# Turning attention probabilities with transposing DMAs, as two 16-bit planes, in a decoder layer on one core

## The chip, the core and the metric

The kernel runs on one core of a Trainium2 chip. The metric is the device time of one launch in microseconds (us). A core has TensorE (PE in the profile), VectorE (DVE), ScalarE (ACT), GpSimd (POOL) and SyncE (SP); each works through its own instructions in order, and the engines wait for each other through semaphores. DMAs are issued by an engine's queue and moved by 16 DMA engines that all queues share.

## The reference, cut to what matters

The program is one decoder layer on x (4 x 512 x 512, float32): a first attention over features, a layer norm, a second attention block, a layer norm, a feed-forward part with ternary weights, and a last layer norm. The change lies in the second block, whose core is this:

```python
def _gqa(q, k, v):
    scale = 1.0 / np.sqrt(q.shape[-1])
    scores = jnp.einsum('bsghd,btgd->bghst', q, k) * scale
    p = jax.nn.softmax(scores, axis=-1)
    return jnp.einsum('bghst,btgd->bsghd', p, v)
```

It is called with 8 groups of 2 heads of width 128 over 512 positions (self-attention), and once more over 64 context positions (cross-attention). Queries and keys come out of linears on 8-bit inputs and a layer norm over each head; both results are divided, rounded to 8-bit values and multiplied by a projection.

## The kernel before, in words

The program has three stages in a row: the first attention with the preparation of the weights, the second block, and the feed-forward part.

**Units and slots.** The second block runs as 16 units: 4 batches times 4 pairs of groups (`u`, lines 1088 to 1130). A unit has 4 heads of 512 query rows, and a head is taken in 4 blocks of 128 rows, so a unit has 16 slots and the block has 256. The whole order of the work is written out by hand: the engines' instructions stand in the order in which the code calls them (only SyncE's DMAs are placed by the scheduler).

**What one slot does for its own block of scores.** `score` (line 818) multiplies 128 query rows with 512 keys into a PSUM tile `ps`, and VectorE takes the row maximum `nm` (line 826). `exponents` (828) lets ScalarE write `p = exp(ps - max)` and the row sums `rsum`. `quotients` (833) takes the reciprocal on VectorE and scales `p` on GpSimd (835). `turn_score` (837), two slots later, turns `p` on TensorE: four transposes of 128 x 128 float32 into a PSUM tile `pt` (line 115, by way of `transpose4`), and ScalarE copies it into `pT` (842). When a head's four blocks are turned, `value` (844) multiplies `pT` with the values in 8 matmuls into `po`, in the third slot of the next head, and `finish` (854) has ScalarE scale the result into a bfloat16 tile `fq_y`, which VectorE rounds to 8-bit values in five steps (lines 207 to 212).

**What else a slot does.** `plan(u)` (1025) puts other work into the slots: the 12 linears of the next unit (`LINEARS`; line 788, 8 or 16 matmuls each), turns of the normalised queries and keys through PSUM (`turn`, line 807, copied by ScalarE in 811), the cross-attention (`CONTEXT`: scores in line 880, its turn, its values in 917), the projection of the unit before (`OUT`, line 946, 8 matmuls each), and, in two of four units, the next batch's inputs (`quantise`, 244). `statistics` (722) and `scale` (735) normalise what the linears left in PSUM: VectorE's statistics, GpSimd's power (109), VectorE's product (740).

**Order on the engines.** In a slot, ScalarE first does the copies that the slot before left in `early`, then the copy of the turned probabilities, then the exponents, then what the plan adds. GpSimd does the quotients and then the powers of `statistics`.

**Buffers.** The PSUM pools hold 4 banks for products, 2 for turns and 2 for scores. The linears' weights come from DRAM in tiles of 512 KB, four to a linear kind (line 773), into 8 buffers, so that a kind's loads start as soon as the kind two before it is done.

Of the kernel before, what the change touches and what calls it, by code (L numbers as in the profile page):

```python
# [28 lines left out]
P = 128  # L29
# [25 lines left out]
def decoder_layer(  # L55
# [79 lines left out]

    fqp = hat = lnp = quants = ps_mm = ps_t = ps_s = None
# [79 lines left out]
    class Inputs:  # L216
# [27 lines left out]
        def quantise(self, w, c0, due=1):  # L244
            def begin():
                if c0 == 0:
                    self.qa[w] = quants.tile([P, KC, S], F32R, name="qa", tag="qa")
                y = fqp.tile([P, 2 * S], BF16, name="fq_y", bufs=4)
                for j in range(2):
                    col = 4 * w + c0 + j  # L250
                    nc.scalar.activation(
                        y[:, j * S : (j + 1) * S], self.lns[c0 + j], AF.Copy,
                        scale=inv_t[:, col : col + 1],
                    )
                round_later(y, self.qa[w][:, c0 : c0 + 2, :].rearrange("p c s -> p (c s)"), due)

            early.append(begin)
# [436 lines left out]
    hatk = wts = qkp = vals = prob = probT = cross = catq = wpp = raws = None  # L694
    turned_as = {0: ("qT", 5), 1: ("qxT", 4), 2: ("kT", 4)}
    parts = 1

    def open_attention(stack, right, wl, v, p, pt, cq, wp, raw):
        nonlocal hat, hatk, wts, qkp, vals, prob, probT, cross, catq, wpp, raws, ps_mm, ps_t, ps_s
        wts = pool_in(right, "wts", wl, **R)  # L700
        qkp = pool_in(stack, "qkp", 4, **L)
        vals = pool_in(stack, "vals", v, **L)
        prob = pool_in(stack, "prob", p, **L)
        probT = pool_in(stack, "probT", pt, **L)
        cross = pool_in(stack, "cross", 2, **L)
        catq = pool_in(stack, "catq", cq, **L)
        wpp = pool_in(stack, "wpp", wp, **L)
        hat = pool_in(stack, "hat", 8 if raw else 4, **L)
        hatk = pool_in(stack, "hatk", 4, **L) if raw else hat
        if raw:  # L710
            raws = pool_in(stack, "raws", 1, **L)
        ps_mm = pool_in(stack, "ps_mm", 4, space=PSUM)
        ps_t = pool_in(stack, "ps_t", 2, space=PSUM)
        ps_s = pool_in(stack, "ps_s", 2, space=PSUM)

    st = ExitStack()
    open_attention(st, right, 8, 10, 4, 1, 6, 1, True)
# [40 lines left out]
    class Unit:  # L758
# [78 lines left out]
        def turn_score(self, i, p):  # L837
            if i == 0:
                self.pT = probT.tile([P, TPB, S], F32, name="pT")
            pt = ps_t.tile([P, 4, P], F32, name="pt", tag="pt")  # L840
            transpose4(pt, p, ident)
            nc.scalar.copy(self.pT[:, :, i * P : (i + 1) * P], pt)  # L842
# [11 lines left out]
        def finish(self, half, j, h, po):  # L854

            if h == 0:
                self.half[half] = fqp.tile([P, 2 * S], BF16, name="fq_y", bufs=4)
# [167 lines left out]
    def plan(u):  # L1025
# [12 lines left out]
        if u == 0:  # L1038
            for j in range(1, 4):
                add(j, me.turn, 0, j)  # L1040
        else:
            add(0, me.turn, 0, 3)
            for j in range(4):
                add(1 + j, me.turn, 1, j)
# [3 lines left out]
        for j, (l, a, t, v) in enumerate(CONTEXT):  # L1048
            add(l, me.load_context, j)
            add(a, me.context_scores, j)  # L1050
            add(t, me.context_turn)
            add(v + (not nxt), me.context_values, j)
        if last:
            if nxt:
                add(1, last.load_out)
            last.pp = {}

            for i, s in enumerate(OUT if nxt else (5, 9)):
                add(s, last.out, i, PAIRS)
# [5 lines left out]
        if me.gp == GP - 2 and b < B:  # L1065
# [3 lines left out]
            quants_at = ((6, 2, 0, 3), (8, 2, 2, 3), (10, 3, 0, 3), (12, 3, 2, 2), (14, 0, 0, 5))  # L1069
        elif me.gp == GP - 1 and b < B:  # L1070
            quants_at = ((2, 0, 2, 3), (4, 1, 0, 3), (7, 1, 2, 3))
# [8 lines left out]
        (0, 2, 0), (1, 2, 1), (3, 2, 2), (5, 2, 3), (7, 0, 0), (8, 0, 1), (9, 0, 2), (11, 0, 3),  # L1080
        (12, 1, 0), (13, 1, 1), (13, 1, 2), (15, 1, 3),
    )
    TURNS = (9, 2, 0), (10, 2, 1), (13, 0, 0), (14, 0, 1), (15, 0, 2)
    CONTEXT = (1, 4, 8, 9), (6, 8, 12, 13)
    OUT = 5, 7, 9, 11
    scored = []
    heads = []
    for u in range(NU):
# [4 lines left out]
        for s in range(16):  # L1093
# [4 lines left out]
            if i == 2 and heads:  # L1098
                me.exponents()
                m, k = heads.pop(0)  # L1100
                m.value(k)
            if len(scored) == 2:
                m, *k = scored.pop(0)
                m.turn_score(*k)
            if i != 2 or u + h == 0:
                me.exponents()
            scored.append((me, i, me.p))
# [5 lines left out]
            me.quotients()  # L1113
            statistics()
            later.run(0.9)
            later.slot += 1
            if u == NU - 1 and s == 0:
# [5 lines left out]
                catq_end = pool_in(right, "catq_end", 4, **R)  # L1123
# [5 lines left out]
            if u == NU - 1 and s == 3:  # L1129
# [4 lines left out]
    for n, (m, *k) in enumerate(scored):  # L1134
        m.turn_score(*k)
        last.out(2 + n, PAIRS)
    later.run(9)
# [178 lines left out]
    with tc.If(rest > 0):  # L1316
# [4 lines left out]
        open_attention(st, st, 4, 4, 2, 1, 2, 2, False)  # L1321
        for b in range(B):
# [9 lines left out]
            for gp in range(GP):  # L1332
# [9 lines left out]
                for j in range(2):  # L1342
                    for h in (2 * j, 2 * j + 1):
                        for i in range(TPB):
# [3 lines left out]
                            me.turn_score(i, me.p)  # L1348
# [89 lines left out]
```

## Time and profile before

| | us |
|---|---|
| median of 3 runs (lowest to highest) | 1772.45 (1772.16 to 1772.91) |
| the profiled execution, its own time | 1770.97 |
| its span, first to last instruction | 1769.1 |
| TensorE busy in the span | 1736.9 |
| VectorE busy | 1216.5 |
| ScalarE busy | 855.6 |
| GpSimd busy | 655.5 |
| first score of the second block starts at | 399.8 |
| granted TensorE clock, mean | 0.998 |

A line of the profile that describes a group of instructions gives the kernel's line, engine, operation, the tiles written and read, the shape, the count after an x, then busy time in us and the mean ns of one, then the idle time of the engine just before them and what ended it. A line of a timeline gives start and length in us, engine, line, operation, tiles, shape and how many follow each other. Matmuls overlap, so what one costs is read from its start to the start of the next. A line of stretches gives, for a piece of the span, each engine's busy time and count, the granted clock, the share of the 16 DMA engines that was busy, and GB/s.

### The profile page before, as it was taken

The page shows a single profiled execution, that of the slowest core. Times are in us where ns is not written, and L with a number is a line of the kernel's source. Part 1 is how long each engine was busy: PE and PEld are TensorE (multiplying, and loading weights), DVE is VectorE, ACT ScalarE, POOL GpSimd, SP SyncE. Part 2 cuts the span into 40 slices and gives each one's busy share as a digit, 9 for nine tenths or more (in the row PEclk, how much of TensorE's full clock was granted, in tenths as well). Part 3 has the DMA queues.
Part 4 walks back from the last instruction along what each step waited for, and adds up shares of the span by engine and source line. Part 5 has one row for each costly group of instructions (what it writes and reads, how often), then busy time and mean ns, then how long its engine had stood idle before and what let it go on. Part 6 is the DMA issues. An engine that isn't in the chain of part 4 may idle for free. (4 is left out here: it accounts for less than half of the span.)

```text
span 1769.1 us, 23876 instructions
## 1 busy us (share of the span) xinstructions
PE 1736.9 (98%) x7874; PEld 1068.3 (60%) x7874; DVE 1216.5 (69%) x2564; ACT 855.6 (48%) x1735; POOL 655.5 (37%) x918
## 2 busy tenths in 40 slices
PE   8999989999999999999999999999999999999997
PEld 4545454466767666666766766666666766644443
DVE  1456666756666886666688676668867675659886
ACT  1445454525545555454555545556554555543221
POOL 1222131333433443343443343334434333326663
PEclk9999999999999999999999999999999999999999
DMA  8768586783433324353232435313342542505543
GB/s 262 225 221 276 158 281 207 231 287 111 134 129 106 123 69 147 115 189 97 103 123 70 148 139 172 137 55 124 104 157 95 172 140 71 201 2 121 122 102 83
DMA packets 161605, 256.91 MB, mean 145 GB/s; under 512 B 60592, under 2 KB 95408, under 8 KB 159424
## 3 DMA queue, kind: packets, MB, share of 16 engines
q1 hardware_dynamic: 160256, 251.06, 43.8%
q0 software_dynamic: 1216, 4.23, 0.8%
q8 instruction: 65, 1.06, 0.2%
q14 instruction: 68, 0.56, 0.1%
HBM read 194.55 MB, written 50.33 MB: 138 GB/s over the span
## 5 line engine op out<-in xcount | busy, mean ns | idle before, releaser
L835 POOL TENSOR_SCALAR p<-p,rsum 128x512 f32<-128x512 f32 x256 | 191.1, 746 | 580.4 <-DVE rsum L834 447.6
L788 PE MATMUL pl<-wl,qa 128*128 128x512 f32 (+1 forms) x2048 | 400.8, 345 | 0.8 <-DVE x L404 0.8
L788 PEld LDWEIGHTS pl<-wl,qa 128*128 128x128 f32 x2048 | 310.2, 189 | 37.0 <-DVE x L404 1.6
L826 DVE TENSOR_REDUCE nm<-ps 128x1 f32<-128x512 f32 x256 | 176.2, 688 | 222.2 <-PE ps L821 222.1
L842 ACT COPY pT<-pt 128x512 f32<-128x512 f32 x256 | 150.5, 588 | 286.8 <-PE pt L115 286.4
L821 PE MATMUL ps<-kT,qT 128*128 128x512 f32 x512 | 265.9, 601 | 4.6 <-ACT p L831 3.7
L831 ACT ACTIVATE p<-ps,nm 128x512 f32<-128x512 f32 x256 | 178.1, 696 | 144.2 <-DVE nm L826 140.6
L109 POOL TENSOR_TENSOR rstd<-rstd,nhalf 128x4 f32<-128x4 f32 (+2 forms) x236 | 226.5, 960 | 19.7
L848 PE MATMUL po<-pT,val 128*128 128x512 f32 x512 | 230.3, 592 | 0.0
L115 PEld LDWEIGHTS pt<-ident,p 128*128 128x128 f32 x1152 | 143.5, 141 | 140.0 <-issue 117.3
L115 PE MATMUL pt<-ident,p 128*128 128x128 f32 x1152 | 172.4, 273 | 1.0 <-POOL p L835 1.0
L848 PEld LDWEIGHTS po<-pT,val 128*128 128x128 f32 x512 | 96.2, 190 | 123.3 <-issue 111.7
L729 DVE BATCH_NORM_STATS2 qk_st<-pl 128x6 f32<-128x256 f32 x320 | 122.8, 419 | 37.5 <-ACT val L796 26.4
L740 DVE TENSOR_TENSOR xn<-pl,rstd 128x512 f32<-128x512 f32 (+1 forms) x192 | 113.3, 595 | 16.9 <-POOL rstd L109 16.5
L946 PE MATMUL pp<-wb,cq 128*128 128x512 bf16 x512 | 121.0, 380 | 0.0
L493 POOL TENSOR_TENSOR wr<-wr,wb 128x512 f32<-128x512 f32 x32 | 38.6, 1207 | 164.6 <-ACT wb L491 118.2
L807 PE MATMUL pt<-ident,xn 128*128 128x128 f32 x640 | 96.1, 273 | 2.9 <-ACT qxT L811 2.6
L821 PEld LDWEIGHTS ps<-kT,qT 128*128 128x128 f32 x512 | 81.5, 190 | 28.4 <-issue 12.6
L1225 ACT ACTIVATE h<-pg,xi_ds 128x512 f32<-128x512 f32 x64 | 43.9, 688 | 109.9 <-PE pg L1220 109.9
L860 ACT ACTIVATE fq_y<-po,inv_t 128x512 bf16<-128x512 f32 x128 | 84.5, 688 | 8.7 <-PE po L848 4.6
L1220 PEld LDWEIGHTS <-xiT 128*128 128x128 bf16 x512 | 50.0, 98 | 61.9 <-issue 1.0
L946 PEld LDWEIGHTS <-cq 128*128 128x128 bf16 x512 | 45.6, 98 | 65.3 <-issue 18.7
(518 smaller groups left out, 2648.7 us busy)
## 6 DMA issues: line engine op xcount, KB each, us to landing
wl<-wl_d SPq DMA_DIRECT2D x192, 512.0 KB, 6.1
wl_d<-wd SPq DMA_DIRECT2D x48, 512.0 KB, 4.4
wb<-wb_d SPq DMA_DIRECT2D x16, 1024.0 KB, 9.5
wr<-in_wproj_dram SPq DMA_DIRECT2D x32, 256.0 KB, 4.5
wr<-in_wgu_dram SPq DMA_DIRECT2D x32, 256.0 KB, 4.8
wr<-in_wqkv_dram SPq DMA_DIRECT2D x32, 256.0 KB, 4.1
raw<-in_wgu_dram SPq DMA_DIRECT2D x32, 256.0 KB, 3.9
tern_d<-tern SPq DMA_DIRECT2D x48, 128.0 KB, 2.2
```

Source lines behind the costliest of these rows:

```text
L109: nc.gpsimd.tensor_tensor(y, y, nhalf[:, :n], ALU.pow)
L115: nc.tensor.transpose(dst[:, c, :], src[:, c * P : (c + 1) * P], idn)
L729: nc.vector.bn_stats(stt[:, 2 * j : 2 * j + 2, :].rearrange("p a b -> p (a b)"), ps[:, 2 * j * D : (2 * j + 2) * D].rearrange("p (h d) -> ...
L740: nc.vector.tensor_tensor(xn, ps[:, : n * D].rearrange("p (h d) -> p h d", h=n), y.unsqueeze(2).broadcast_to([P, n, D]), ALU.mult,)
L788: nc.tensor.matmul(ps[:, at : at + n], lhsT=self.qa[a][:, c, ts], rhs=self.ws[c][:, k, at : at + n], start=(c == 0 and k == 0), stop=(c == ...
L821: nc.tensor.matmul(self.ps, lhsT=self.qT[h][:, i * P : (i + 1) * P], rhs=self.kT[h // 2], start=True, stop=True,)
L826: nc.vector.tensor_reduce(self.nm, self.ps, AX.X, ALU.max, negate=True)
L831: nc.scalar.activation(self.p, self.ps, AF.Exp, bias=self.nm, accum_out=self.rs)
L835: nc.gpsimd.tensor_scalar(self.p, self.p, self.rs, 1.0, ALU.mult, ALU.mult)
L842: nc.scalar.copy(self.pT[:, :, i * P : (i + 1) * P], pt)
L848: nc.tensor.matmul(po, lhsT=self.val[c][:, j * D : (j + 1) * D], rhs=self.pT[:, c, :], start=(c == 0), stop=(c == TPB - 1),)
L946: nc.tensor.matmul(pp, lhsT=q, rhs=w, start=(first and n == 0), stop=(last and n == len(terms) - 1))
```

## The change

The four transposes and their PSUM tile go away for the probabilities. In `quotients`, GpSimd now also copies `p`, read as 16-bit halves, into a tile `p2` with the 512 low halves first and the 512 high halves behind them. `send`, a slot later, is a transposing DMA of the 128 x 1024 16-bit values into `t2`, issued from ScalarE's queue. `receive`, two slots after that, is a ScalarE copy that joins the two planes again in `pT`: 1024 16-bit elements in place of 512 float32. `value` stands in the fourth slot of the next head, where it stood in the third. The plan's slots are laid out anew, and some buffer counts change: weights 8 to 7, values 10 to 11, `p` 4 to 2, `qT` 5 to 4, `kT` 4 to 3, the last projection's inputs 4 to 2. The computation is the same.

```diff
-    turned_as = {0: ("qT", 5), 1: ("qxT", 4), 2: ("kT", 4)}
+    turned_as = {0: ("qT", 4), 1: ("qxT", 4), 2: ("kT", 3)}
...
+        planes = pool_in(stack, "planes", 2 if raw else 1, **L)
...
-    open_attention(st, right, 8, 10, 4, 1, 6, 1, True)
+    open_attention(st, right, 7, 11, 2, 1, 6, 1, True)
...
             nc.gpsimd.tensor_scalar(self.p, self.p, self.rs, 1.0, ALU.mult, ALU.mult)
 
-        def turn_score(self, i, p):
+            self.p2 = planes.tile([P, 2, S], U16, name="p2")
+            nc.gpsimd.tensor_copy(self.p2, self.p.bitcast(U16).rearrange("p (k h) -> p h k", h=2))
+
+        def send(self, p2):
+
+            t2 = planes.tile([P, 2 * TPB, P], U16, name="t2", bufs=3 if parts == 1 else 1)
+            nc.scalar.dma_start(t2, p2.rearrange("p h k -> p (h k)"), transpose=True)
+            return t2
+
+        def receive(self, i, t2):
+
             if i == 0:
                 self.pT = probT.tile([P, TPB, S], F32, name="pT")
-            pt = ps_t.tile([P, 4, P], F32, name="pt", tag="pt")
-            transpose4(pt, p, ident)
-            nc.scalar.copy(self.pT[:, :, i * P : (i + 1) * P], pt)
+            nc.scalar.copy(
+                self.pT[:, :, i * P : (i + 1) * P].bitcast(U16).rearrange("p c (q h) -> p c q h", h=2),
+                t2.rearrange("p (h c) q -> p c q h", h=2),
+            )
...
-            quants_at = ((6, 2, 0, 3), (8, 2, 2, 3), (10, 3, 0, 3), (12, 3, 2, 2), (14, 0, 0, 5))
+            quants_at = ((6, 2, 0, 2), (8, 2, 2, 2), (10, 3, 0, 2), (12, 3, 2, 1), (14, 0, 0, 4))
         elif me.gp == GP - 1 and b < B:
-            quants_at = ((2, 0, 2, 3), (4, 1, 0, 3), (7, 1, 2, 3))
+            quants_at = ((0, 0, 2, 2), (3, 1, 0, 3), (5, 1, 2, 2))
...
     LINEARS = (
-        (0, 2, 0), (1, 2, 1), (3, 2, 2), (5, 2, 3), (7, 0, 0), (8, 0, 1), (9, 0, 2), (11, 0, 3),
-        (12, 1, 0), (13, 1, 1), (13, 1, 2), (15, 1, 3),
+        (0, 2, 0), (1, 2, 1), (2, 2, 2), (4, 2, 3), (5, 0, 0), (6, 0, 1), (8, 0, 2), (9, 0, 3),
+        (10, 1, 0), (12, 1, 1), (13, 1, 2), (14, 1, 3),
     )
-    TURNS = (9, 2, 0), (10, 2, 1), (13, 0, 0), (14, 0, 1), (15, 0, 2)
-    CONTEXT = (1, 4, 8, 9), (6, 8, 12, 13)
-    OUT = 5, 7, 9, 11
+    OWN = (0, 0, 3), (1, 1, 0), (2, 1, 1), (3, 1, 2), (4, 1, 3)
+    TURNS = (7, 2, 0), (11, 2, 1), (13, 0, 0), (14, 0, 1), (15, 0, 2)
+
+    CONTEXT = (1, 5, 10, 14), (9, 13, 18, 20)
+    CONTEXT_END = (1, 5, 9, 10), (6, 9, 13, 15)
+    OUT = 8, 9, 10, 12
     scored = []
+    sent = []
     heads = []
+
+    def move_on():
+        while scored:
+            m, i, p2 = scored.pop(0)
+            sent.append((m, i, m.send(p2)))
...
-            if i == 2 and heads:
-                me.exponents()
+            if i == 3 and heads:
                 m, k = heads.pop(0)
                 m.value(k)
-            if len(scored) == 2:
-                m, *k = scored.pop(0)
-                m.turn_score(*k)
-            if i != 2 or u + h == 0:
-                me.exponents()
-            scored.append((me, i, me.p))
+            me.exponents()
+            arrived = sent[:-1]
+            del sent[:-1]
+            move_on()
+            for m, k, t2 in arrived:
+                m.receive(k, t2)
...
             me.quotients()
+            scored.append((me, i, me.p2))
...
     run_early()
-    for n, (m, *k) in enumerate(scored):
-        m.turn_score(*k)
+    for n in range(2):
+        move_on()
+        m, k, t2 = sent.pop(0)
+        m.receive(k, t2)
         last.out(2 + n, PAIRS)
+    for m, k, t2 in sent:
+        m.receive(k, t2)
     later.run(9)
     me.value(3)
```

A triple of `LINEARS` is (slot, kind, block), where kind 2 gives keys and values, 0 the queries and 1 the cross-attention's queries; `OWN` and `TURNS` are (slot, kind, head). A row of `CONTEXT` gives the slots of its load, scores, turn and values; numbers from 16 up lie in the next unit.

More of the change, by code (lines that the diff above doesn't have):

```diff
@@ L134, in decoder_layer @@
     nc.vector.tensor_copy(ident_h, ident)
+    parts = 1
     fqp = hat = lnp = quants = ps_mm = ps_t = ps_s = None
@@ L247, in begin @@
                     self.qa[w] = quants.tile([P, KC, S], F32R, name="qa", tag="qa")
-                y = fqp.tile([P, 2 * S], BF16, name="fq_y", bufs=4)
+                y = fqp.tile([P, 2 * S], BF16, name="fq_y", bufs=4 if parts == 1 else 2)
                 for j in range(2):
@@ L691, in decoder_layer @@
     left.close()
-    hatk = wts = qkp = vals = prob = probT = cross = catq = wpp = raws = None
-    turned_as = {0: ("qT", 5), 1: ("qxT", 4), 2: ("kT", 4)}
-    parts = 1
+    hatk = wts = qkp = vals = prob = probT = cross = catq = wpp = raws = planes = None
+    turned_as = {0: ("qT", 4), 1: ("qxT", 4), 2: ("kT", 3)}
     def open_attention(stack, right, wl, v, p, pt, cq, wp, raw):
-        nonlocal hat, hatk, wts, qkp, vals, prob, probT, cross, catq, wpp, raws, ps_mm, ps_t, ps_s
+        nonlocal hat, hatk, wts, qkp, vals, prob, probT, cross, catq, wpp, raws, planes, ps_mm, ps_t, ps_s
         wts = pool_in(right, "wts", wl, **R)
@@ L856, in finish @@
             if h == 0:
-                self.half[half] = fqp.tile([P, 2 * S], BF16, name="fq_y", bufs=4)
+                self.half[half] = fqp.tile([P, 2 * S], BF16, name="fq_y", bufs=4 if parts == 1 else 2)
             y = self.half[half]
@@ L1036, in plan @@
                 add(s, nxt.linear, w, i)
[L1038 to L1044, printed above, removed]
+        for s, w, j in OWN if u > 0 else ((0, 0, 1), (1, 0, 2), (2, 0, 3)):
+            add(s, me.turn, w, j)
         if nxt:
@@ L1047, in plan @@
                 add(s, nxt.turn, w, j)
-        for j, (l, a, t, v) in enumerate(CONTEXT):
+        if last:
+            add(CONTEXT[1][2] - 16, last.context_turn)
+            add(CONTEXT[1][3] - 16, last.context_values, 1)
+        for j, (l, a, t, v) in enumerate(CONTEXT if nxt else CONTEXT_END):
             add(l, me.load_context, j)
             add(a, me.context_scores, j)
-            add(t, me.context_turn)
-            add(v + (not nxt), me.context_values, j)
+            if t < 16:
+                add(t, me.context_turn)
+                add(v, me.context_values, j)
         if last:
@@ L1056, in plan @@
             last.pp = {}
-            for i, s in enumerate(OUT if nxt else (5, 9)):
+            for i, s in enumerate(OUT if nxt else (8, 12)):
                 add(s, last.out, i, PAIRS)
@@ L1122, in decoder_layer @@
                 wpp = pool_in(right, "wpp_end", 1, **R)
-                catq_end = pool_in(right, "catq_end", 4, **R)
+                catq_end = pool_in(right, "catq_end", 2, **R)
                 me.load_out()
@@ L1128, in decoder_layer @@
                     (gu if k < 8 else dn).append(t)
-            if u == NU - 1 and s == 3:
+            if u == NU - 1 and s == 12:
                 catq = catq_end
@@ L1320, in decoder_layer @@
         open_inputs(st, st)
-        open_attention(st, st, 4, 4, 2, 1, 2, 2, False)
+        open_attention(st, st, 4, 4, 1, 1, 2, 2, False)
         for b in range(B):
@@ L1347, in decoder_layer @@
                             me.quotients()
-                            me.turn_score(i, me.p)
+                            me.receive(i, me.send(me.p2))
                         me.value(h)
```

## Prediction

> **What bounds the kernel now.** I read first the busy times over the 256 slots, then TensorE's timeline in one slot, then the groups of the other engines, then the one kind of transposing DMA that this kernel already has. Busy time in stretches: the second block's middle, then a light unit and one of the heavy ones that also prepare a batch.
>
> ```profile
> core 0: us, PE busy (x) PEld busy (x) DVE busy (x) ACT busy (x) POOL busy (x), PEclk, DMA share, GB/s
> 420.00:1540.00 1120.00, 1115.50 (x5578) 746.53 (x5577) 798.08 (x1712) 604.88 (x1207) 443.25 (x632) 1.00 0.36 123
> 464.70:540.00 75.30, 75.30 (x379) 50.35 (x378) 47.74 (x104) 38.70 (x79) 28.33 (x43) 1.00 0.37 124
> 540.00:616.80 76.80, 76.80 (x394) 51.82 (x393) 59.32 (x125) 44.61 (x87) 31.50 (x44) 1.00 0.30 108
> ```
>
> TensorE has no gap; nobody else is near full. The four kinds of unit take 75.3, 76.8, 76.5 and 75.3 us, mean 76.0; ScalarE has 41.2 of it (38.7, 44.6, 42.6, 38.8), VectorE 55.2, GpSimd 30.3. Whether "busy" is work is seen from start to start on TensorE:
>
> ```profile
> 812.08 3.60 PE L848 MATMUL po<-pT,val 128*128 128x512 f32 x8
> 815.51 0.60 PE L115 MATMUL pt<-ident,p 128*128 128x128 f32 x4
> 815.95 0.60 PE L807 MATMUL pt<-ident,xn 128*128 128x128 f32 x4
> 816.39 1.02 PE L821 MATMUL ps<-kT,qT 128*128 128x512 f32 x2
> 817.25 0.60 PE L115 MATMUL pt<-ident,p 128*128 128x128 f32 x4
> 817.61 2.10 PE L788 MATMUL pl<-wl,qa 128*128 128x512 f32 x8
> 819.55 1.90 PE L946 MATMUL pp<-wb,cq 128*128 128x512 bf16 x8
> 821.28 1.02 PE L821 MATMUL ps<-kT,qT 128*128 128x512 f32 x2
> ```
>
> Scores cost 0.86, a linear 1.94 (2.0 in 16 matmuls), a projection 1.73, a value 3.43, a turn of queries or keys 0.44, cross scores 1.73, cross values 1.07. A turn of probabilities costs 0.36 ahead of a linear and 0.44 elsewhere. A unit's sum is 16x0.86 + 4x2.0 + 8x1.94 + 4x3.43 + 4x1.73 + 10x0.44 + 2x(0.44+1.73+1.07) = 68.8, and 6.2 for ten turns at 0.36 and six at 0.44: 75.0 against 75.3 measured. So the block is TensorE's work and nothing else.
>
> **What is removed.** 256 turns: 160x0.36 + 96x0.44 = 100 us of TensorE. The profiled execution took 1771.0 (span 1769.1 and 1.9 around it; the median is 1.5 above). If TensorE stayed full, 1671. The question is what is late in its place.
>
> **What is added, on whom.**
>
> ```profile
> L1187 POOL TENSOR_SCALAR hi_i<-h 128x1024 bf16<-128x1024 f32 x31 | 32.4, 1044 | 2.6
> L835 POOL TENSOR_SCALAR p<-p,rsum 128x512 f32<-128x512 f32 x256 | 191.1, 746 | 580.4 <-DVE rsum L834 447.6
> L842 ACT COPY pT<-pt 128x512 f32<-128x512 f32 x256 | 150.5, 588 | 286.8 <-PE pt L115 286.4
> L1248 SPq DMA_TRANSPOSE hiT<-hi_i x32: 1231/1232/2041, 1606.8 to 1755.0; - x32
> DMA to landing us min/median/max: 3.0/3.2/4.8
> 1680.90:1684.00 3.10, 3.10 (x16) 1.44 (x15) 2.90 (x8) 1.07 (x3) 2.71 (x4) 1.00 0.44 85
> ```
>
> *GpSimd's split* (1024 16-bit elements) was not run before. Nearest row: L1187, 1024 elements in 1.04; I take 1.05, with 0.9 and 2.1 (twice, if a step of two halves the rate) as ends. 16 of them make GpSimd 30.3 + 16.8 = 47 of some 70 us: hidden. It stands ahead of the powers of `statistics`, which come 1.05 later; VectorE's product waits for them at the start of the next slot, behind the row maximum, which is not there before 0.86 + 0.7 = 1.6 either. GpSimd also meets VectorE more often: L835 takes 691 at least and 746 on average, and VectorE's bfloat16 sums (L211) 674 at least and 784 on average in the block. With GpSimd busy 67% and not 40%, the like stretching of some 3.6 us a unit on VectorE becomes 6: VectorE 57.6 of 70, 64 in heavy units.
>
> *ScalarE's join* reads two places 1 KB apart in turn. Rows: a copy of 256 elements (L796) takes 372, one of 512 588, so 0.84 ns an element and 1.02 us for 1024; twice the slope, if each alternating read misses, gives 1.9. I take 1.02, nearest to the row: +0.43 a slot.
>
> *The DMA.* The same size, 128 x 1024 of 16 bits, is moved in the feed-forward part. Its issue holds the queue 1.23 us, it lands 3.2 us after its start, and in the stretch with one alone the 16 DMA engines are busy 0.44 of 3.1 = 1.36 us. The Trainium skill (VectorE: DVE Perf Modes, "The three transpose paths" and the rules after it) speaks against the change: 390 ns for a 128x128 bfloat16 block on TensorE, 1309 ns through the DMA, and TensorE where PSUM will do. By that, 8 blocks are 10.5 us in a slot of 4.35, and the block would take over 2600 us. By the row, eight blocks take 3.2 together, beside other work, and TensorE's block costs 0.11, not 0.39; the measurement decides. The DMA share rises from 0.36 by 1.36/4.35 to about 0.7.
>
> *The issue on ScalarE's queue* has no row: no DMA is issued there before. Lower end: nothing, if ScalarE computes what was queued while its sequencer issues. Upper end: 1.23 of dead time a slot. The trace leans to the lower: of 515 semaphore instructions of ScalarE's sequencer, 279 lie wholly inside a running compute instruction. The Trainium skill (Advanced Engine Details and Errata, "Sequencer Loop") says so too: other engine instructions can be queued while such a control instruction executes. But the issue stands behind the exponents, with 0.9 us queued ahead of it, and the join, the copies of turns and `val` are queued behind it; so I charge 1.23 - 0.9 = 0.33. It waits for `p2`: exponents end about 2.7 into a slot, then reciprocal, quotient 0.75 and split 1.05, so `p2` is there some 1 us into the next slot, ahead of that slot's exponents.
>
> ScalarE then has 41.2 + 16x(0.43 + 0.33) = 53.4 of 70: hidden on average. In the lightest slots (0 and 1: TensorE 0.86 + 2.0 + 0.44 = 3.3; 6: 2.8) it has up to 4, and lags by about 1 us.
>
> *Latency.* Issue to join is two slots, 8.7 us on average, against 3.2 landing. A kind's weights are four loads of 512 KB (6.1 us median to landing); between those a transpose takes longer, at most about their whole 6 us plus its own 1.4 and 1.2 of issue, 8.6: just in time. The last join of a head ends about 3.9 into slot 2 (3.7 long), and the value wants it 0.86 into slot 3: 0.6 to spare; I charge 0.5 a unit.
>
> *Seven weight buffers.* The fourth tile of the queries' weights now waits for the first tile of the keys', last used in slot 4 (about 2.2 in), and is wanted in slot 5 after 0.86 + 3x0.48: 4.4 us later. A first load of a burst lands in 3.4 to 3.8 after its issue in this trace, later beside a transpose. I charge 0.5 a unit (0 to 2). The other two kinds have over 5 us. The remaining buffers and the slots' new order I cost at nothing: the same matmuls, and VectorE (at most 64 of 70) covers them; without that cover they would show as lag, which I charge at 1.5 a unit with GpSimd's stretching.
>
> *The end.* Unit 15 has little TensorE work, and TensorE waits for ScalarE there already; its 6.2 is not gained. The last value waits for split, issue, landing and join (1.05 + 3.2 + 1.02) where it waited for a turn and a copy (1.0); two projections (3.5) cover both. I charge 3.
>
> **Sum.** 1671 + 15 units x (0.5 + 0.5 + 1.5) + 6 + 3 = 1717.5; with the median's 1.5, 1719, or 3% faster.
>
> **The rivals.**
> *A: nothing is late.* 1671 and the end's 9: 1680 to 1695. For it: GpSimd and ScalarE have room. Against it: slots of 3.3 us with 4 us of ScalarE. Chance 0.10.
> *B: the issue holds ScalarE, the join is at its lower end.* 41.2 + 16x(0.43 + 1.23) = 67.8 against TensorE's 69.7: two nearly full engines that wait for each other in uneven slots, some 74 a unit, 15x2 = 30 gained: 1742, and up to 1768. Against it: the 279. Chance 0.14.
> *C: late transposes.* DMAs at 0.7 share come in bursts; 2 us late behind each of three bursts is 6 us a unit, all of the gain: 1769 to 1776. Chance 0.04.
> *D: slower, ScalarE is the bound.* The issue holds it 1.23 and the join takes 1.9 (1.31 more): 41.2 + 16x2.54 = 81.8 a unit, 5.8 over 76.0, 1772 + 15x5.8 = 1859. It turns slower once the addition passes (76.0 - 41.2)/16 = 2.17 us a slot. For it: both costs have no row of their own, and a sequencer that waits for `p2` holds back everything behind it. Chance 0.26, from 1776 to 1860.
> The forecast, 1695 to 1742, has 0.46.
>
> A measurement of this kernel tells a change of about 0.2% from none. Faster is A, the forecast and B: 0.70; same C: 0.04; slower D: 0.26. The range leaves out the lowest part of A (0.03) and the upper part of D (0.15): 1683 to 1805. The forecast's own range is 1695 to 1742.
>
> **What would show it.** In the changed profile: no group L115 with `p`; TensorE full in the heavy slots (values, cross scores) and short gaps in slots 0, 1, 5 and 6; units of about 72 us. ScalarE's join at 1.0 and GpSimd's split at 1.05 (1.9 and 2.1 would be the upper ends). The DMA issue on ScalarE's queue at 1.23 with compute running inside it; if the copies always start after its end, B or D. Transposes landing in 3 to 5 us, with few joins waiting for them; if "DMA t2" ends much of ScalarE's idle time, C. A wait for a weight load ahead of L788 in slot 5 shows the seven buffers. I am wrong if ScalarE's or GpSimd's busy time comes near the unit's length.

## The result, and the profile after

The changed kernel takes 1884.8 us (median of 4 runs, 1882.95 to 1887.79) where the kernel before took 1772.31 beside it: a ratio of 1.0644, 95% interval 1.063 to 1.0657, or 6.4% slower. The forecast was 1719 with a range up to 1805, so it was wrong in sign and in size. The profiled execution took 1887.8 us, with a span of 1886.0 against 1769.1: 116.9 us more. By the starts of the scores these lie here:

| stretch | before, us | after, us | more |
|---|---|---|---|
| up to the first score | 399.8 | 403.5 | 3.7 |
| unit 0 | 61.2 | 69.0 | 7.8 |
| units 1 to 14 (one of them) | 1063.2 (75.9) | 1144.0 (81.7) | 80.8 |
| unit 15, up to its last score | 49.6 | 63.1 | 13.5 |
| from there to the last `po` | 10.3 | 21.5 | 11.2 |
| the rest | 185.1 | 185.0 | -0.1 |

The busy times of the stretch that the prediction shows of the kernel before, of unit 5 with a little of unit 6, and of units 1 to 14:

```profile
core 0: us, PE busy (x) PEld busy (x) DVE busy (x) ACT busy (x) POOL busy (x), PEclk, DMA share, GB/s
420.00:1540.00 1120.00, 1003.92 (x4267) 618.17 (x4268) 785.77 (x1591) 677.67 (x1109) 640.08 (x806) 0.95 0.68 165
796.20:876.90 80.70, 74.27 (x326) 46.16 (x325) 52.48 (x112) 49.30 (x82) 47.45 (x61) 0.96 0.83 196
472.40:1616.40 1144.00, 1027.85 (x4418) 633.17 (x4417) 807.35 (x1633) 697.23 (x1141) 655.16 (x824) 0.95 0.68 163
```

Units 1 to 14 of the kernel before:

```profile
461.00:1524.20 1063.20, 1059.68 (x5315) 709.47 (x5314) 761.20 (x1634) 571.61 (x1140) 421.75 (x600) 1.00 0.35 120
```

TensorE now has gaps, and no other engine has taken its place: ScalarE is busy 61% of the time, GpSimd 57%, VectorE 70%. Over units 1 to 14, TensorE was busy 1059.7 us before and 1027.9 after. The turns taken away are worth 14 x 6.25 = 87.5 us, so its busy time should have fallen to 972; 55.7 of the gain went into a longer busy time. In the trace the granted clock is 0.50 for 112 us of these units, and TensorE is busy in some 91 of them; half of that, some 45 us, is my estimate of the clock's part in the 55.7. The idle time rose from 3.5 to 116.2. So -87.5 + 112.7 of idle + 55.7 of longer work = 80.9, the table's 80.8.

Both are seen in one slot. Below, TensorE in slots 2 and 3 of unit 5 in the changed kernel:

```profile
802.85 1.02 PE L822 MATMUL ps<-kT,qT 128*128 128x512 f32 x2
803.31 2.48 PE L789 MATMUL pl<-wl,qa 128*128 128x256 f32 x16
805.62 0.60 PE L808 MATMUL pt<-ident,xn 128*128 128x128 f32 x4
810.31 1.09 PE L115 MATMUL pt<-ident,p 128*128 128x128 f32 x4 [4.09 <-ACT qxT L812]
811.19 1.91 PE L822 MATMUL ps<-kT,qT 128*128 128x512 f32 x2
813.56 5.03 PE L860 MATMUL po<-pT,val 128*128 128x512 f32 x8 [0.46 <-ACT pT L851]
```

TensorE stands 4.09 us for a ScalarE copy (`qxT`) that frees a PSUM buffer for turns. After that a score pair takes 1.91 where it took 1.02, and a value 5.03 where it took 3.6. The stretches of the same time give the granted clock:

```profile
796.00:806.00 10.00, 10.00 (x71) 8.55 (x69) 7.36 (x16) 5.97 (x11) 7.58 (x10) 1.00 1.05 230
806.00:809.40 3.40, 0.22 (x3) 0.00 (x0) 1.66 (x5) 2.12 (x5) 1.58 (x2) 1.00 1.24 331
809.50:816.20 6.70, 5.43 (x9) 2.43 (x10) 3.69 (x9) 5.30 (x10) 3.71 (x7) 0.50 0.30 62
816.30:822.00 5.70, 5.70 (x32) 3.98 (x30) 2.07 (x6) 3.08 (x5) 1.73 (x2) 1.00 0.47 112
```

The clock is 1.00 up to 809.4, late in the gap that began at 806.2, then 0.50 for 6.8 us, then 1.00 again. In units 1 to 14 this happens 19 times, for 3.4, 6.8 or 10.2 us, always 1.7 to 4.4 us after the start of a gap of TensorE of 1.3 to 4.9 us; in the same units of the kernel before it never happens. So a stall of this kind is paid again in part after its end.

Why was that copy late? ScalarE and VectorE in slots 1 and 2 (a line with ACTq is the issue of the DMA, on ScalarE's sequencer):

```profile
801.02 0.69 ACT L832 ACTIVATE p<-ps,nm 128x512 f32<-128x512 f32 x1 [1.94 <-DVE nm L827]
801.31 1.28 ACTq L844 DMA_TRANSPOSE t<-p  x1
801.60 0.19 ACT L832 ACTIVATION_READ_ACCUMULATOR p<-ps,nm 128x1 f32 x1
802.63 1.16 ACT L851 COPY pT<-t 128x1024 uint16<-128x1024 uint16 x1 [0.84 <-issue]
803.70 0.37 ACT L797 COPY val<-pl 128x256 f32<-128x256 f32 x1
803.96 0.79 ACT L812 ACTIVATE qT<-pt,qp_t 128x512 f32<-128x512 f32 x1
806.68 0.69 ACT L832 ACTIVATE p<-ps,nm 128x512 f32<-128x512 f32 x1 [1.93 <-DVE nm L827]
```

```profile
804.10 0.43 DVE L730 BATCH_NORM_STATS2 qk_st<-pl 128x6 f32<-128x256 f32 x1 [2.11 <-ACT val L797]
804.45 0.41 DVE L205 TENSOR_SCALAR fq_m<-fq_y 128x1024 uint16<-128x1024 uint16 x1
804.89 0.43 DVE L210 TENSOR_SCALAR fq_m<-fq_m 128x1024 bf16<-128x1024 bf16 x1
805.35 0.69 DVE L212 TENSOR_TENSOR fq_y<-fq_y,fq_m 128x1024 bf16<-128x1024 bf16 x1
805.96 0.68 DVE L827 TENSOR_REDUCE nm<-ps 128x1 f32<-128x512 f32 x1
```

Read it as a ring. The exponents wait for the row maximum. The issue starts 0.29 us after them, when GpSimd's split for the slot before has ended (801.27), and ends 0.8 us after the row sums are read out; the join waits for it; the copy `val` waits behind the join; VectorE's statistics wait 2.11 for `val`; and the next row maximum stands behind the statistics and three steps of the rounding on VectorE, so the next exponents wait 1.93 for it. From exponents to exponents 5.66 us pass, in a slot in which TensorE has 3.2 of work. ScalarE idles in it twice and is nowhere near full. The groups that carry this, and the last two of them in the kernel before:

```profile
L851 ACT COPY pT<-t 128x1024 uint16<-128x1024 uint16 x256 | 297.9, 1165 | 266.2 <-issue 125.9
L839 POOL COPY p<-p 128x1024 uint16<-128x1024 uint16 x256 | 277.8, 1085 | 47.4 <-DMA t<-p 32.0
L741 DVE TENSOR_TENSOR xn<-pl,rstd 128x512 f32<-128x512 f32 (+1 forms) x192 | 115.4, 601 | 189.5 <-POOL rstd L109 189.2
L730 DVE BATCH_NORM_STATS2 qk_st<-pl 128x6 f32<-128x256 f32 x320 | 122.9, 417 | 104.0 <-ACT val L797 96.1
```

```profile
L740 DVE TENSOR_TENSOR xn<-pl,rstd 128x512 f32<-128x512 f32 (+1 forms) x192 | 113.3, 595 | 16.9 <-POOL rstd L109 16.5
L729 DVE BATCH_NORM_STATS2 qk_st<-pl 128x6 f32<-128x256 f32 x320 | 122.8, 419 | 37.5 <-ACT val L796 26.4
```

Joins stand 266 us, 126 of it behind the issue. VectorE's product stands 189 us for GpSimd's powers (16.5 before), which now come behind the split, and its statistics 96 us for `val` (26 before). GpSimd closes a second ring: split, powers, product, row maximum.

The slots' mean lengths over units 1 to 14, worked out from the starts of the scores:

```
slot      0   1   2   3   4   5   6   7   8   9   10  11  12  13  14  15  unit
after     3.4 3.6 8.1 8.0 4.4 4.7 4.0 6.3 4.5 4.4 5.0 5.7 4.6 5.2 4.5 5.3 81.7
slots     3.7 3.6 4.4 5.2 4.8 5.1 3.3 5.4 5.0 4.9 5.3 5.2 4.9 5.3 4.8 5.3 76.0
powers+SP 3.2 3.2 4.0 5.9 4.4 6.9 3.3 5.0 4.5 4.4 6.2 4.8 4.4 4.9 4.3 4.8 74.5
```

The second row is the run with TensorE's turns in the new slots, the third the run with the powers first and SyncE's queue, both below. Slots 2 and 3 hold over half of what the changed kernel loses; most others are at TensorE's own work.

### The profile page after: what moved, and what is told of

Same layout as the page of the kernel before. It is cut to its first block, busy times and chain, and to the rows that moved or that the text cites. A ratio compares the mean times of both kernels' runs of the same rounds, so it can differ in the third digit from the quotient of the medians.

```text
span 1886.0 us, 22128 instructions
## 1 busy us (share of the span) xinstructions
PE 1711.1 (91%) x6850; PEld 987.0 (52%) x6850; DVE 1265.9 (67%) x2564; ACT 998.9 (53%) x1735; POOL 923.9 (49%) x1174
## 4 chain that ended last, share of the span: by engine, by line
POOL 25%; PE 18%; issue 17%; DVE 9%; DMA 8%; ACT 6%; ACTq 2%; POOLq 0%; SPq 0%; DVEq 0%
POOL p L839 9%; POOL rstd L109 8%; DMA t<-p 6%; POOL p L836 5%; PE po L860 5%; ACT pT L851 4%; PE pd L1279 3%; PE pu L1245 3%; POOL rstd L108 3%; PE pg L1245 3%; ACTq L844 2%; PE pl L789 2%; PE pp L958 1%; DVE xn L741 1%; DVE fq_y L212 1%
## 5 line engine op out<-in xcount | busy, mean ns | idle before, releaser
L789 PE MATMUL pl<-wl,qa 128*128 128x512 f32 (+1 forms) x2048 | 466.4, 375 | 12.5 <-DMA wl<-wl_d 8.3
L851 ACT COPY pT<-t 128x1024 uint16<-128x1024 uint16 x256 | 297.9, 1165 | 266.2 <-issue 125.9
L789 PEld LDWEIGHTS pl<-wl,qa 128*128 128x128 f32 x2048 | 325.7, 191 | 137.2 <-issue 72.9
L836 POOL TENSOR_SCALAR p<-p,rsum 128x512 f32<-128x512 f32 x256 | 181.2, 708 | 399.7 <-DVE rsum L835 395.0
L822 PE MATMUL ps<-kT,qT 128*128 128x512 f32 x512 | 287.5, 645 | 34.0 <-ACT p L832 33.0
L860 PE MATMUL po<-pT,val 128*128 128x512 f32 x512 | 266.7, 669 | 48.0 <-ACT pT L851 47.8
L839 POOL COPY p<-p 128x1024 uint16<-128x1024 uint16 x256 | 277.8, 1085 | 47.4 <-DMA t<-p 32.0
L109 POOL TENSOR_TENSOR rstd<-rstd,nhalf 128x4 f32<-128x4 f32 (+2 forms) x236 | 216.7, 918 | 19.7
L808 PEld LDWEIGHTS pt<-ident,xn 128*128 128x128 f32 x640 | 77.7, 141 | 42.8 <-issue 33.6
L212 DVE TENSOR_TENSOR fq_y<-fq_y,fq_m 128x1024 bf16<-128x1024 bf16 x96 | 89.6, 934 | 1.7
```

Of the source, the lines that this page charges most:

```text
L109: nc.gpsimd.tensor_tensor(y, y, nhalf[:, :n], ALU.pow)
L789: nc.tensor.matmul(ps[:, at : at + n], lhsT=self.qa[a][:, c, ts], rhs=self.ws[c][:, k, at : at + n], start=(c == 0 and k == 0), stop=(c == ...
L808: nc.tensor.transpose(pt[:, i, :], self.xn[w][i][:, j, :], ident)
L822: nc.tensor.matmul(self.ps, lhsT=self.qT[h][:, i * P : (i + 1) * P], rhs=self.kT[h // 2], start=True, stop=True,)
L836: nc.gpsimd.tensor_scalar(self.p, self.p, self.rs, 1.0, ALU.mult, ALU.mult)
L839: nc.gpsimd.tensor_copy(self.p2, self.p.bitcast(U16).rearrange("p (k h) -> p h k", h=2))
```

## Experiments

Each time is a median of timed runs, with its ratio to the kernel before run beside it.

**The layout alone.** TensorE turns again, in the new slots.

```diff
-            self.p2 = planes.tile([P, 2, S], U16, name="p2")
...
+            self.p2 = self.p
...
+            pt = ps_t.tile([P, 4, P], F32, name="pt", tag="pt")
+            transpose4(pt, t2, ident)
+            nc.scalar.copy(self.pT[:, :, i * P : (i + 1) * P], pt)
```

> The changed kernel's slots, unit plan and buffer counts, with the probabilities turned on TensorE again (no split, no DMA, joins replaced by the copy out of PSUM). If the ring of waits through the added split, issue and join is the cause (theory 1), TensorE is full again and the time is near the kernel before: 1770 to 1800 us, unit mean 75.5 to 77. If the new order of the slots and the smaller buffers are the cause (rival: layout), it stays at 1840 or more and slots 2 and 3 stay 3 us too long.

1786.7 us, ratio 1.0078 (1.006 to 1.0096); unit mean 76.0, as the first theory expected. The layout is not the cause of the loss in the units; it costs some 15 us elsewhere. Of the 17.4 us by which its profiled span is longer, 9.1 lie ahead of the first score (which comes at 402 to 409 us in these runs, whatever the edit), 6.2 behind the last score, and 1.3 in units 1 to 14.

**SyncE issues the transposes.**

```diff
-            nc.scalar.dma_start(t2, p2.rearrange("p h k -> p (h k)"), transpose=True)
+            nc.sync.dma_start(t2, p2.rearrange("p h k -> p (h k)"), transpose=True)
```

> Only the queue of the transposing DMA changes: SyncE issues it in place of ScalarE. Theory 1 (a ring: row maximum, exponents, rest of the issue, join, copy of the values, statistics, next row maximum): 0.6 us less in each turn of the ring in five slots of a unit and before some joins, so 40 to 60 us less: 1825 to 1845. Rival (the issue on ScalarE is the whole cause): ScalarE's 126 us of idle behind the issue go, 1740 to 1770. Rival (late transposes): SyncE holds loads back behind the wait for the planes, no gain or slower, 1880 to 1920.

1840.8, ratio 1.0382 (1.0358 to 1.0407): 44 us less than the changed kernel, inside the first theory's range. `val` comes in time again (40.5 us of waits, 86.0 in the changed kernel from 475 to 1600 us), but the product's wait for the powers stays at 174, and TensorE now waits for weights:

```profile
DVE xn L741 <- POOL rstd L109: 174.2, 144, 3.3
...
DVE qk_st L730 <- ACT val L797: 40.5, 44, 1.2
PEld pl L789 <- DMA wl<-wl_d: 37.1, 23, 4.5
```

**A shorter join.** The low halves are left out.

```diff
-            nc.scalar.copy(
-                self.pT[:, :, i * P : (i + 1) * P].bitcast(U16).rearrange("p c (q h) -> p c q h", h=2),
-                t2.rearrange("p (h c) q -> p c q h", h=2),
-            )
+            nc.scalar.copy(self.pT[:, :, i * P : (i + 1) * P], t2[:, TPB:, :].bitcast(BF16))
```

> The join copies only the high plane (512 elements as bfloat16, so the low halves of the probabilities are left out); split, DMA and slots stay. Join 0.59 in place of 1.165 us, ScalarE 147 us less busy in all. Theory 1: the ring is 0.58 shorter, 35 to 55 us less: 1830 to 1850. Rival (ScalarE's sum is the bound, 53 per cent busy): hardly anything, since its busy time is no bound; if it were, 16 times 0.58 a unit, 1735.

1860.9, ratio 1.0483 (1.0449 to 1.0518). ScalarE lost 134 us of busy time (998.9 to 864.8) and the kernel 24: less than the first theory's 35 to 55, and far from what a full ScalarE would give.

**The join last in its slot.**

```diff
-            for m, k, t2 in arrived:
-                m.receive(k, t2)
...
             for f in pl[s]:
                 f()
+            for m, k, t2 in arrived:
+                m.receive(k, t2)
```

> The join is moved behind the copies that the plan adds in its slot, so that the copy of the values and the statistics behind it no longer wait for 1.16 us of join. Theory 1: slots 0, 1, 2 and 4 lose 0.5 to 1.1 us each, slot 2 most; 40 to 60 us less, some of it given back since the last join of a head ends later before its value: 1825 to 1855. If GpSimd's split or the transposes' landing is the cause, within 10 us of 1885.

1878.3, ratio 1.0608 (1.058 to 1.0635): a miss for the first theory, and what was expected if the split or the landing is the cause. The statistics' wait for `val` fell from 89 to 24 us (420 to 1600 us), but the product's wait for the powers rose from 182 to 224: taking one wait away lengthened the other.

**The powers ahead of the split.**

```diff
             me.quotients()
-            scored.append((me, i, me.p2))
             statistics()
             later.run(0.9)
+            me.part()
+            scored.append((me, i, me.p2))
```

`part` holds the split.

> GpSimd's split stands behind the powers of the statistics in place of ahead of them; nothing else changes. VectorE's products wait 182 us for those powers in the units (before: 17), and the next row maximum stands behind them. Theory 1 (a ring of in-order waits in which GpSimd's split has a part): most of the 182 goes, and where nothing else is late, half of the loss: unit 81.7 to about 77.5, 1815 to 1840. Rival (ScalarE's issue and join alone make the loss): less than 15 us, 1870 or more, since the split ends later and the planes with it.

1895.1, ratio 1.0692 (1.0657 to 1.0726): a miss in sign for the first theory, and what the rival expected. The waits of this run, from 475 to 1600 us:

```profile
ACT pT L853 <- issue: 136.2, 118, 2.5
...
DVE qk_st L730 <- ACT val L797: 105.3, 55, 4.5
...
DVE xn L741 <- POOL rstd L109: 35.4, 82, 1.0
```

The product's wait fell from 169 to 35 as expected. But the split, now later, is what ScalarE's queue waits for. Of the 224 issues of units 1 to 14, the split held back some 60 to 80 beyond their turn on the queue in the changed kernel, 60 to 70 us in all, and 140 to 170 here, 170 to 200 us in all; the counts depend on where an issue's turn is taken to begin.

**No split.** The quotient goes into a bfloat16 high plane, the low plane is zero, so the low halves are left out.

```diff
+                self.p2 = halves[count[0] % 2]
+                count[0] += 1
+                nc.gpsimd.tensor_scalar(self.p2[:, 1, :].bitcast(BF16), self.p, self.rs, 1.0, ALU.mult, ALU.mult)
```

> No split at all: GpSimd's quotient is written as bfloat16 into the high plane of two standing tiles whose low plane is zero (so the low halves of the probabilities are left out); DMA, issue and join keep their size. GpSimd 278 us less busy and the planes 1.05 us earlier. Theory 1: like the run with the powers first, and some more, 1805 to 1835. Rival (issue and join alone): 1865 or more. If it comes down to 1790, the split alone was the cause and the issue and the join are harmless.

1813.9, ratio 1.022 (1.0176 to 1.0264), inside the first theory's range: 71 us of the change's 113 go with GpSimd's split, though GpSimd was busy only 49% of the span; issue and join are as long as ever. 194 us of waits of GpSimd for the transposes that still read the two standing tiles are this run's own.

**Powers first and SyncE's queue**, the two edits together.

> Powers first, and SyncE issues the transposes. Theory 1 expects the two gains to add or more, since each loosens another piece of the same ring: 44 from the queue and 45 to 70 from the powers, 1770 to 1800, with waits for weight loads on TensorE left (77 us in the run with SyncE alone). Rival (either is enough for the ring): no better than the better of the two alone, 1815 to 1840.

1778.0, ratio 1.0037 (1.0018 to 1.0055). Alone, the queue gave 44 and the powers lost 10; together they give 107. The engines' work is what it was (units 1 to 14; ScalarE 683.30 and GpSimd 649.76, 697.23 and 655.16 in the changed kernel):

```profile
467.00:1510.70 1043.70, 990.66 (x4391) 627.37 (x4417) 788.38 (x1633) 683.30 (x1141) 649.76 (x825) 0.98 0.71 179
```

With the issue off ScalarE's queue a late split no longer holds up a computing engine, and the powers can go first. Waits for the weights and the powers that are left (475 to 1600 us), and then SyncE's queue, waiting for the split:

```profile
PEld pl L789 <- DMA wl<-wl_d: 43.7, 25, 4.5
...
PE pl L789 <- DMA wl<-wl_d: 33.0, 25, 4.1
DVE xn L741 <- POOL rstd L109: 28.5, 53, 1.9
```

```profile
SPq L846 <- POOL p L841: 287.2, 162, 4.0
```

The hold is not gone, then; it has moved to a queue that also carries the weights. In units 1 to 14 TensorE stands over 0.4 us for a weight tile 21 times, and each time that tile was issued straight behind a transpose, and landed in the 4.0 to 6.5 us that a tile takes here.

**An unread transpose in the kernel before.** Nothing is left out; the transpose and its buffer are added.

```diff
+            if scored:
+                t2 = prob.tile([P, 2 * TPB, P], U16, name="t2", bufs=1)
+                nc.scalar.dma_start(t2, scored[-1][2].bitcast(U16), transpose=True)
```

> The kernel before, with one addition: behind the exponents of each slot ScalarE issues a transposing DMA of the same size from the probabilities of the slot before, into a tile that nobody reads (the buffers of p go from 4 to 3 to make room). TensorE still turns the probabilities. It prices the issue and the traffic alone. Theory 1: ScalarE has 41 of 76 us a unit, 0.6 of issue stands open in a slot and TensorE's own work covers it: 1772 to 1790. Rival (issue or traffic is the cause by itself): 1820 or more. Late loads of weights would show as waits of TensorE for DMA.

2135.7, ratio 1.2089 (1.2052 to 1.2127): on the rival's side by the number, but not for the rival's reason. The one tile `t2` makes each issue wait for the landing before it: 179 of 254 issues start within 0.2 us of it. ScalarE's row in this run:

```profile
878.52 0.19 ACT L831 ACTIVATION_READ_ACCUMULATOR p<-ps,nm 128x1 f32 x1
885.96 1.30 ACTq L1109 DMA_TRANSPOSE t<-p  x1
887.30 0.37 ACT L796 COPY val<-pl 128x256 f32<-128x256 f32 x1 [8.59 <-issue]
```

The profile puts all 8.59 us down to "issue", of which 1.30 is the issue and the rest a wait at the head of the queue. It is the plainest view here of what a DMA that waits on a computing engine's queue costs.

**The same with a transpose that need not wait**, two slots old, into two tiles.

```diff
+            if old and u < NU - 1:
+                t2 = wts.tile([P, 2 * TPB, P], U16, name="t2", bufs=2)
+                nc.scalar.dma_start(t2, old[0].bitcast(U16), transpose=True)
```

> The kernel before, with an unread transposing DMA behind each slot's exponents, as in the run that took 2136, but from the probabilities of two slots earlier and into two tiles by turns (weights in 7 buffers to make room; none in unit 15), so that its issue hardly waits. Theory 2 (a wait at the head of the queue costs, not the issue or the traffic): near the kernel before, 1772 to 1800, where the run with one tile waited for the landing before in 179 of 254 issues. Rival (issue length or traffic): 1900 or more.

1831.6, ratio 1.0348 (1.0329 to 1.0366): between the two. Most of the earlier loss went; 59 us stay. The quietest units take 76.3 to 76.8 where a light unit took 75.3; the others lose up to 12 in slots 2 to 5, where the exponents wait for a late transpose to have read their buffer (46.8 us of waits).

**Sent a slot later**, joined one slot after that.

```diff
-            arrived = sent[:-1]
-            del sent[:-1]
-            move_on()
+            arrived = sent[:]
+            del sent[:]
+            move_on(1)
```

> The transpose is sent a slot later and joined one slot after that in place of two, so score to join takes as long as before (three plane tiles and two transposed ones in place of two and three); ScalarE still issues it. Theory 2, formed after the first eight runs (what costs is the issue's wait for the split, at the head of ScalarE's in-order queue: 66 of 217 issues start after the exponents have ended, up to 5.5 us): the issue finds its planes ready, the long stalls in slots 2 and 3 go, 1780 to 1820; some joins now wait for their landing of 3 to 4 us. Theory 1 in its first form (the issue's own length and the join in the ring): no gain, 1875 to 1900. Rival (late transposes): slower, over 1900.

1931.5, ratio 1.0918 (1.0877 to 1.0958).

The second run also puts the powers first:

> Sent a slot later, and GpSimd's split behind the powers. With the issue on ScalarE and the planes only just in time, powers first gained nothing (1895). Theory 2: with the wait of the issue gone, powers first gains what it gained with SyncE's queue (63 us there): 1740 to 1780. Rival (the two queues differ by the issue's own 1.25 us on ScalarE): 1800 to 1840.

1919.9, ratio 1.0853 (1.0813 to 1.0893).

The third also puts the join last:

> Sent a slot later, powers first, and the join behind the plan's copies of its slot, so that a join that waits for its landing, or for the value that still reads the turned tile, holds up nothing but itself. Theory 2: the best of the three, 1725 to 1765, TensorE waiting only in slot 3 and in unit 15. Rival (TensorE waits for the last join of a head): no better than the run before it in this list.

1875.2, ratio 1.0595 (1.0574 to 1.0617). All three missed the second theory's range; the first lies where its rival, late transposes, put it. The split hardly held an issue back any more (some 5 us in all), so that hold alone is not the cause. But the joins had one slot to wait for the landing, and it was not enough. Of the run with powers first:

```profile
ACT pT L853 <- DMA t<-p: 131.8, 50, 10.9
```

So the late transposes, which hardly show in the changed kernel because of its two slots, are real. Landing after issue over the 224 transposes of units 1 to 14: on ScalarE's queue beside SyncE's loads median 3.6 us, 28 over 7, longest 13.0 (changed kernel), median 4.1, 47 over 7, longest 15.7 (sent later with the powers first); on SyncE's queue with the loads median 3.1, none over 7 (the changed kernel with SyncE's queue, and the same with the powers first). These runs trade one wait for another, and do not price the hold by itself.

**The last weight tiles from ScalarE's queue, and the join last**, both on top of powers first and SyncE's queue.

```diff
+                q = nc.scalar if w < 2 and c == KC - 1 and self.ahead else nc.sync
+                q.dma_start(ws[c].bitcast(F32), wl_d[self.gp, w, c])
```

The weight tiles alone:

> As the run with the powers first and SyncE's queue (1778), but the last weight tile of the queries and of the cross-attention's queries, whose buffer comes free only a slot before its use, is loaded from ScalarE's queue at the end of slot 4 or 9, behind no transpose. If late weights are what remains (slot 5: 6.9 where TensorE's work is 4.5, slot 10: 6.2 where it is 4.9), 3 to 3.5 us a unit go: 1725 to 1740, close to the forecast of 1719. If those slots wait for something else, 1770 to 1780.

1771.4, ratio 0.9991 (0.9974 to 1.0009): what was expected if those slots wait for something else. Slot 10 came down from 6.2 to 5.1, slot 5 stayed at 6.9.

The join last alone:

> Powers first, SyncE's queue, and the join behind the plan's copies; loads as in the changed kernel. If the ring through the join and the copy of the values still decides, 15 to 30 us under the run without the move: 1750 to 1765. If the ring was broken by the other two, within 8 us of 1778, or a little slower where a late join meets its value in slot 3.

1765.8, ratio 0.9965 (0.9946 to 0.9983): 12 us for the move that gave 7 in the changed kernel; slots 2 and 3 are now 3.9 and 5.2.

Both:

> Both: the last weight tiles from ScalarE's queue and the join behind the plan's copies. If the two are separate causes, their gains add: 1715 to 1735. If only the weights remain, the same as the first run of this list within 8 us.

1763.0, ratio 0.9942 (0.992 to 0.9965): 15 us together, not far from the sum of the two (7 and 12), and far from the 1715 to 1735 expected of it.

**The cross-attention's weights later as well.**

```diff
+                if s == 4:
+                    add(4, nxt.preload, 0, 0, 1, 2, 3)
+                if s == 6:
+                    add(6, nxt.preload, 1, 0, 1, 2)
+                if s == 9:
+                    add(9, nxt.preload, 1, 3)
```

> Powers first, SyncE's queue, the join last, the queries' last weight tile from ScalarE's queue in slot 4, and the first three tiles of the cross-attention's queries only in slot 6, the last in slot 9, also from ScalarE's queue. If the loads that burst beside the urgent one are what remains, slot 5 falls from 8.0 to 4.5 to 5.5 and the unit from 74.3 to 71 to 72: 1720 to 1740. If the queue order or the transposes themselves make it late, slot 5 stays above 6.5 and the time at 1755 to 1770. Unit 15 and the end keep their 20 us of loss either way.

1757.6, ratio 0.9923 (0.9897 to 0.9949): the lowest median, 0.8% under the kernel before, though its interval overlaps with that of the run before it. In its profiled execution units 1 to 14 take 1027.8 us, 35 less than before, and unit 15 and the stretch behind it 19.4 more. Slot 5, as the second of the two expectations had it, did not come down: it is still 6.9 on average: 4.6 to 6.3 in most units, 8.5 to 13.2 in four. In the worst one, TensorE:

```profile
785.70 1.22 PE L796 MATMUL pl<-wl,qa 128*128 128x512 f32 x2 [6.33 <-DMA wl<-wl_d]
```

and the issues on the two queues shortly before:

```profile
775.07 1.24 SPq L853 DMA_TRANSPOSE t<-p  x1
776.98 0.46 SPq L894 DMA_DIRECT2D vx<-vx_d  x1
```

```profile
775.52 0.39 ACTq L782 DMA_DIRECT2D wl<-wl_d  x1
```

The transpose landed 10.8 us after its issue and the weight tile 10.1 after its own, though only a second transpose and two loads of 32 KB were issued in the meantime. The DMA engines were busy throughout, at little throughput:

```profile
775.50:785.60 10.10, 3.87 (x16) 1.85 (x14) 5.32 (x12) 5.13 (x8) 4.02 (x5) 0.86 1.16 132
768.00:774.50 6.50, 6.50 (x26) 3.55 (x25) 2.40 (x6) 5.11 (x9) 3.88 (x6) 1.00 1.10 355
```

The second line is a stretch of the same unit in which transposes and loads all came from SyncE's queue: about the same DMA share (1.10 against 1.16), and 355 GB/s in place of 132. My cause, a burst of loads, is out for these units; that transposes and loads meet from two queues fits. Two pairs of runs come near to trying it by itself, since they differ only in the queue of the last weight tiles and in the slot in which their kind's loads are called: with 28 of them in units 1 to 14 in place of none, 4 transposes in place of none landed over 7 us after their issue (1771.4 against 1778.0), and 6 in place of none with the join last (1763.0 against 1765.8); in this run, with 70, it was 18. What makes them slow each other is not shown.

## Why the prediction was wrong

**The step that failed** is the one that compares sums. For ScalarE it reads "ScalarE then has 41.2 + 16x(0.43 + 0.33) = 53.4 of 70: hidden on average", for GpSimd's split "GpSimd 30.3 + 16.8 = 47 of some 70 us: hidden", and the split's place ahead of the powers was put at nothing. The busy times came out: ScalarE 697.2 over 14 units is 49.8, against 41.2 + 16 x 0.43 = 48.1, and GpSimd 655.2 / 14 is 46.8. What failed is "hidden". The prediction named what stands behind the issue ("the join, the copies of turns and `val` are queued behind it") and did not ask who waits for `val`: VectorE's statistics do (96 us), as its product waits for the powers (189 us); the next row maximum is behind these, and the next exponents behind that. In a ring, no engine has to be full, so its sign of being wrong, ScalarE's or GpSimd's busy time near the unit's length, did not show either. That order and queue decide and not the sums is what the run with the powers first and SyncE's queue shows: with nearly the same busy times, 107 of the 113 us are gone. It allowed "lags by about 1 us" in the light slots; slots 2 and 3 alone are on average 7.7 longer than the shortest such slots in the runs with this layout (3.65 and 4.78).

**The rest, by its own steps.**
- *Turns removed, 100 us:* the instructions are gone, and over units 1 to 14 87.5 us should follow; 55.7 of them went into a longer busy time, most of it at a lower clock after stalls. No term of the sum was for that.
- *Split 1.05:* 1.085. Its place ahead of the powers was costed at nothing, because the product stands behind a row maximum that was not ready either. The product waited 189 us for the powers.
- *Join 1.02:* 1.165. The upper end of 1.9 was not it.
- *Issue, 0.33 exposed:* the issue took 1.25 as predicted, but it starts 0.1 to 0.3 us behind the start of the exponents, which with their row sums take 0.77 in place of 0.9, so some 0.6 to 0.8 is exposed. And `p2` is not always there "some 1 us into the next slot, ahead of that slot's exponents": in the slot shown above the split ends 1.6 us into it, and these holds make another 60 to 70 us of waits at the queue.
- *Landing 3.2, at most 8.6:* median 3.6, longest 13. In the changed kernel two slots hide most of it.
- *VectorE, 57.6 a unit:* 807.35 / 14 = 57.7. Right, and not what decided.
- *Seven weight buffers, 0.5:* not seen in the changed kernel (slot 5 at 4.7), nor in the layout run, which has seven too. TensorE waits for weights when SyncE's queue carries the transposes as well (slot 5 at 6.9).
- *The end, 6.2 not gained and 3 more:* unit 15 and what follows lost 13.5 + 11.2 = 24.7. The layout run loses 7.4 there, and 18.5 stay with the powers first and SyncE's queue; which wait makes the rest is not worked out.

**The rivals.** D ended on the right side, at 1859, but its mechanism, a full ScalarE, is one that the runs reject: ScalarE was busy 49.8 of 81.7 us, and with 134 us less of it the kernel gained 24. It did name the sequencer that waits for `p2`. B charged the issue in full, and moving it gave 44 us, but it too had a nearly full ScalarE and no ring. C, late transposes, is what the later runs met.

**My later theories** fell too. The first, a ring, predicted gains from the join's place and from the powers that did not come (7, and -10). The hold of the issue by the split alone predicted gains from sending later that did not come. What stands is the pair: a split ahead of the powers delays VectorE, a split behind them delays ScalarE's queue, and only with the issue on an idle engine's queue can the split be late without holding up a computing engine: 107 of the 113 us. Part of that pair's gain may be the shorter landing on SyncE's queue; these runs do not separate it. Nor is it settled what makes a transpose and a load slow each other from two queues. Two buffers for `pT`, so that the first join of a head need not wait for a value, were not tried.

## What to carry to other kernels

When work moves from a full engine to engines with room, do not compare busy sums; follow, from each added instruction, who waits for what stands behind it on its in-order queue, until the path either ends or comes back to where it began, and compare the length of that ring with the shortest slot. A DMA that waits for another engine belongs on the queue of an engine that computes nothing, and even there not ahead of a load that is needed soon; and an addition on a helper engine belongs behind what others wait for; here each of the two alone gave little or lost, and both together nearly all. Count the clock too: a full TensorE that begins to stall also runs slower afterwards, here at half the clock for 3.4 to 10.2 us.

## What was not expected of the hardware

After a TensorE gap of 4.09 us the granted clock was 0.50 for 6.8 us; in units 1 to 14 of the changed kernel it was at 0.50 for 112 us in all, which made an estimated 45 of the 55.7 us of longer busy time. A transposing DMA of 256 KB landed in 3.1 us in the median when it shared SyncE's queue with 512 KB loads, never over 7.0 in units 1 to 14 of the runs with all of both on that queue, and up to 13 to 17 us when it was issued from ScalarE's queue beside them; once, a single weight tile and a transpose from two queues took 10 us each. VectorE's bfloat16 operation `fq_y<-fq_y,fq_m` (line 211 before, 212 after) took 779 ns before and 966 after, from 475 to 1600 us; with the new layout and no split it took 698 (the layout run) and 701 (the run without a split), so it is the split on GpSimd that goes with the slower VectorE.
